# A gated projection split in twelve-bit parts: when its parts are made, and on which engine

## The chip, the cores and the metric

The kernel runs on one core of a Trainium2 chip. A core has five engines that matter here, each with its own queue of instructions in a fixed order: TensorE (PE in the profile; its weight loads are PEld), VectorE (DVE), ScalarE (ACT), GpSimd (POOL) and SyncE (SP), which issues transfers. TensorE multiplies from SBUF into the eight banks of PSUM; the others move and combine. The metric is the device time of one execution in microseconds (us), lower being better, given as the median of several runs.

## The reference

A graph network over 1024 nodes with 512 features: a normalisation, a graph convolution, four layers, a second graph convolution. What matters here is the second half of each layer:

```python
for i in range(L):                                    # L = 4
    a = _attn(_ln(h, ln2_w[i], ln2_b[i]), cond, Wq[i], Wk[i], Wv[i], Wo[i])
    h = h + a
    u = _ln(h, ln3_w[i], ln3_b[i]) @ geglu_w[i] + geglu_b[i]   # 1024x512 @ 512x4096
    val, gate = jnp.split(u, 2, axis=-1)
    f = val * jax.nn.gelu(gate, approximate=False)
    h = h + f @ ffo_w[i] + ffo_b[i]                            # 1024x2048 @ 2048x512
```

The first product, with `geglu_w`, is the gated projection; the second, with `ffo_w`, is the output product, and `ffo_w` holds the output weights.

## The kernel before

**Parts.** Most products are made in float32r, a matmul type for operands of few bits, in place of plain float32. So each operand is split in three: a high part (the value scaled by a power of two and rounded by the write), a low part (what is left), and a third part that is a combination of both. A product is then three matmuls: high by high and low by low into one bank, that bank scaled by `1 + TINY` on ScalarE or VectorE, and third by third on top.

**Seven products.** The gated projection is taken in blocks of 2 by 2 by a scheme with seven products in place of eight (0 to 6; `SPLIT` and `EARLY` are orders of these seven). The seven left operands are blocks of `geglu_w` and sums of blocks; the seven right operands (`right`) are blocks of the normalised, turned `h` (`ln3T`) and sums of them (`ln3S`). Value and gate halves of the weights are the two block rows, so that one run of seven products gives value and gate together.

**Order of the stage.** The columns of the projection are worked off in 16 units of 128. The first four are `Quad`s (L959), in plain float32, which need no parts. They run while the parts of the seven right blocks are made, one step at a time: `all_parts` (L1644) is a generator that goes over the blocks in the order `EARLY` = 0, 1, 4, 6, 5, 3, 2 and yields after every small step; `fill` (L1661) takes one step. A quad's `rest` (L987) calls its `fill` six times, between its sums on VectorE. For each block `begin_right` (L1022) makes the high part `gr` on ScalarE (L1024), twice a scaled half `gt` on ScalarE (L1027) and from it the third part, also `gr`, on VectorE (L1029); `finish_right` (L1032) makes the low part `gl` in two halves on VectorE (L1037). That is four steps a block.

The other twelve units are `Chunk`s (L1057). A chunk loads its weights (`gxa`, `gxb`), makes its sums of weight blocks on GpSimd (`sums`, L1073, instructions at L1079), and splits the weights (`split_steps`, L1081, through `split_left`, L1040): high parts `gha`, `ghb`, `gs` on ScalarE (L1042), low parts `gla`, `glb`, `gs` on VectorE (L1043), third parts `gsa`, `gsb`, `gs` on GpSimd (L1048). The "long" flow is the part of 128x1024 (`gha`, `gla`, `gsa`), the "short" flow the parts of 128x512 and 128x256. Then `steps` (L1136) does the seven products of three parts (L1107): for products 0, 5, 6 and 4 a scaling on ScalarE (L1121) stands between the second and the third part; for 1, 3 and 2 one on VectorE (L1125). The last steps of a chunk run inside the next chunk's iteration (`before`).

The loop over the chunks (from L1742) also prepares the stage behind it: `Output` (L1200) reads the result `f` back from DRAM (`fetch`), splits it (`split` through `left_parts`, L314: `ah_f` on ScalarE at L318, `al_f` on VectorE at L319, `as_f` on GpSimd at L321 for the first piece), and splits the output weights (`split_w`, L1223: `bh_wff` on ScalarE at L1226, `bl_wff` on VectorE at L1229, `bs_wff` on VectorE at L1233). `ahead` (L1237) runs `split_w` step by step: its first step comes at the end of the fifth chunk's iteration (`n == 0`), the next four in the chunks behind it, the rest in the output product (L1252).

**What sets the order.** A planner orders the instructions of each engine by program order as priority, by its own estimate of when operands and buffers are ready; it may put a later instruction ahead of an earlier one that has to wait. `pin` (L55) keeps pinned instructions in program order among themselves on their engine; `in_order` (L97) ties each instruction traced inside it behind the one traced before it on that engine. Buffers come from pools: 35 slots of 128x1024 (`slots`, L75), ten tiles of 128x512 (`work`, L76), and eight banks; a tile is given out again when its last reader is done.

**Last quad and first chunk.** Before the last quad's `rest`, the first chunk's two flows are begun (high parts), and that quad's six fills are taken from a list, `first_chunk` (L1710). The first chunk's sums are asked for after the second quad, the second chunk's after the third, and the third chunk's inside the first chunk's iteration, through `sum_next` (L1155).

Of the kernel before, what the change touches and what calls it, by code (L numbers as in the profile page):

```python
# [12 lines left out]
F32R = mybir.dt.float32r  # L13
I32 = mybir.dt.int32
AF = mybir.ActivationFunctionType
OP = mybir.AluOpType
# [5 lines left out]
TINY = 2.0 ** -12  # L22
INWARD = 1.0 - 2.0 ** -13
# [3 lines left out]
def gnn_kernel(  # L27
# [26 lines left out]
    nc = tc.nc  # L54
    pin = tc.keep_in_program_order  # L55
# [40 lines left out]
    @contextmanager  # L96
    def in_order(engine):  # L97

        traced = nc.cur_bb.bb.instructions
        n = len(traced)  # L100
        before = next((i for i in reversed(traced) if i.engine == engine), None)
        yield
        for i in traced[n:]:
            if i.engine == engine:
                if before is not None:
                    tc.add_manual_dep(i, before.name, mybir.DependencyInfo(
                        mybir.DependencyClass.NoSync, mybir.DependencyReason.DATA))
                before = i
# [4 lines left out]
    def t512(name, dtype=F32):  # L113
        return work.tile([P, 512], dtype, tag="t512", name=name)

    def slot(name):
        return slots.tile([P, 2, 512], F32, tag="slot", name=name)
# [109 lines left out]
    h = [hall[:, nb, :] for nb in range(NB)]  # L227
# [78 lines left out]
    def twelve_bits(t):  # L306
        return t.bitcast(F32R)
# [103 lines left out]
    def keys(l, g, wk, n=0, by=(0, 1)):  # L411

        to = blocks_in(kTs, g, f"kT_{l}_{g}")
        return [Twelve(f"k_{l}_{g}_{c}", wk, c, conds[g], to(c), by[c % 2]) for c in range(n, KC)]
# [59 lines left out]
    high = gp.tile([ET, P], F32, name="high")  # L474
# [543 lines left out]

    SPLIT = (0, 5, 6, 4, 1, 3, 2)
    EARLY = (0, 1, 4, 6, 5, 3, 2)  # L1020

    def begin_right(name, x, h, s):  # L1022

        nc.scalar.mul(h.bitcast(F32R), x, INWARD / TINY)  # L1024
        for k in range(2):
            more = t512(f"{name}_{k}")
            nc.scalar.mul(more, h[:, k, :], 1.0 + TINY)  # L1027
            yield
            pin(nc.vector.scalar_tensor_tensor(s.bitcast(F32R)[:, k, :], x[:, k, :], 1.0 / TINY,  # L1029
                                               more, OP.mult, OP.subtract))  # L1030

    def finish_right(name, x, h):  # L1032

        low = slot(name)
        for k in range(2):
            yield low
            pin(nc.vector.scalar_tensor_tensor(low.bitcast(F32R)[:, k, :], x[:, k, :], 1.0 / TINY,  # L1037
                                               h[:, k, :], OP.mult, OP.subtract))

    def split_left(x, h, l, s, t):  # L1040

        yield pin(nc.scalar.mul(h.bitcast(F32R), x, INWARD * TINY))  # L1042
        split_left.low = pin(nc.vector.scalar_tensor_tensor(l.bitcast(F32R), h, -1.0 / TINY, x,  # L1043
                                                            OP.mult, OP.add))
        yield split_left.low
        for at in range(0, x.shape[-1], 512):
            h_at, l_at, s_at = (t[:, at:min(at + 512, x.shape[-1])] for t in (h, l, s.bitcast(F32R)))
            split_left.last = pin(t.tensor_tensor(s_at, h_at, l_at, OP.subtract))  # L1048
            yield split_left.last
# [144 lines left out]
    def quads_of(l, r, left, right):  # L1194
        f = Gated(l, r)
        return f, [Quad(l, r, c, left, right, f) for c in range(KC)]
# [3 lines left out]
    class Output:  # L1200
# [22 lines left out]
        def split_w(self, u):  # L1223
            x, name = self.raw_w.pop(u), f"wff_{self.l}_{u}"
            h, l, s = self.w[u] = [slot(f"{n}_{name}") for n in ("bh", "bl", "bs")]
            nc.scalar.mul(twelve_bits(h), x, INWARD / TINY)  # L1226
            yield
            for k in range(2):
                pin(nc.vector.scalar_tensor_tensor(  # L1229
                    twelve_bits(l)[:, k, :], x[:, k, :], 1.0 / TINY, h[:, k, :], OP.mult,  # L1230
                    OP.subtract))
                yield
                pin(nc.vector.scalar_tensor_tensor(  # L1233
                    twelve_bits(s)[:, k, :], h[:, k, :], -TINY, l[:, k, :], OP.mult, OP.add))
                yield
# [155 lines left out]
    def four_wide(name):  # L1391
        return wos.tile([P, 4, 512], F32, tag="wos", name=name)
# [47 lines left out]
    for l in range(L):  # L1440
# [128 lines left out]
        for g in range(NG - 1):  # L1569
# [13 lines left out]
            k = keys(l, g + 1, wk, 1 if l == 0 and g == 0 else 0)  # L1583
# [55 lines left out]
        f, quads = quads_of(l, 0, left, right)  # L1639
# [4 lines left out]
        def all_parts():  # L1644
            for i in EARLY:
                x, name = right[i], f"{l}_{i}"
                if i == 3:
                    wide = four_wide(f"gr_{l}")
                    high, mid = wide[:, :2, :], wide[:, 2:, :]
                else:  # L1650
                    high, mid = slot(f"gr_{name}"), slot(f"gr_{name}")
                yield from begin_right(f"gt_{name}", x, high, mid)
                flow = finish_right(f"gl_{name}", x, high)
                Chunk.rights[i] = high, next(flow), mid
                yield
                for _ in flow:
                    yield

        parts = all_parts()

        def fill(n=1):  # L1661
# [35 lines left out]
        def load():  # L1697
            if chunks:
                ready.append(Chunk(l, *chunks.pop(0)))

        def sum_chunk(n):
            if n < len(ready):
                ready[n].sums()

        def begin_split(n, low, t=nc.gpsimd):
            flow = ready[n].split_steps(low, t) if n < len(ready) else iter(())
            next(flow, None)
            return flow

        first_chunk = []  # L1710
# [5 lines left out]
        for c, q in enumerate(quads):  # L1716
            if c == KC - 1:
                long, short = (begin_split(0, low) for low in (False, True))
                first_chunk.extend([[long] * 3, [short], [short] * 4, [parts], [parts], [parts]])
            q.rest(fill_first if c == KC - 1 else fill)  # L1720
            if c == 0:
                load()
            if c == 1:
                sum_chunk(0)
                load()
            if c == 2:
                sum_chunk(1)
                load()

        def split_rest(short):  # L1730
            long = begin_split(0, False)
            next(long, None)
            with waiting_for(split_left.low, mybir.EngineType.Pool):
                for flow in short, long:
                    for _ in flow:
                        pass

        output = Output(l)
        ahead = output.ahead()
        before, short = None, iter(())  # L1740
        for r in range(1, R):
            f = Gated(l, r)  # L1742
            for c in range(KC):
                n = (r - R + 2) * KC + c
                if n == -1:
                    output.fetch_w(0)
                if (r, c) == (R - 1, KC - 2):
                    output.fetch(0)
                chunk = ready.pop(0)
                flow = chunk.steps(lambda: sum_chunk(1))  # L1750
                chunk.f = f
                next(flow)
                if 0 < n < 5:
                    next(ahead)
                for _ in islice(short, 2):
                    pass
                next(flow)
                if before:
                    split_rest(short)
                    load()  # L1760
                for _ in parts:
                    pass
                if (r, c) == (R - 1, KC - 1):
                    output.split(0, nc.gpsimd)
                    output.fetch(1)
                for step in range(3):
                    if before:
                        next(before, None)
                    next(flow)
                    if step == 1 and not before:  # L1770
                        split_rest(iter(()))
                        load()
                before = flow
                short = begin_split(0, True)
                if n == 0:
                    next(ahead)
# [204 lines left out]
```

## Time and profile before

| | us |
|---|---|
| median of 3 runs | 2312.76 (2312.65 to 2314.91) |
| the profiled execution | 2312.2 |
| its span, first to last instruction | 2310.4 |

| engine | busy, share of the span |
|---|---|
| PE | 99% |
| PEld, DVE | 75% each |
| ACT | 48% |
| POOL | 32% |

The granted TensorE clock was 1.000 over the span. Lines of a timeline give the start in us from the span's start, the duration in us (of all merged instructions), engine, source line, operation, output<-inputs, size and count, and in brackets the idle time of the engine just before with what ended it. Successive matmuls overlap: two of 128x512 last 0.62 us together but the next two start 0.455 later, so lost time is read from starts, not from ends. A row of waits gives the total us, how often, and the longest. A row of windows gives a stretch, its length, then for PE, PEld, DVE, ACT and POOL busy time (instructions), the granted clock, the share of the DMA engines and GB/s. A row of the profile's groups gives the busy time and mean ns of one.

### The profile page before, as it was taken

Reading aid. Unit: us, or ns where it says so; the run is one execution under the profiler, and the core shown is the slowest. Engines: PE = TensorE matmul, PEld = TensorE weight load, DVE = VectorE, ACT = ScalarE, POOL = GpSimd, SP = SyncE. Lnnn points to the kernel's source line nnn. Section 1 sums busy time; section 2 is a strip of 40 time slices with the busy share of each in tenths; the row PEclk is TensorE's granted clock in tenths of the full one; section 3 lists DMA queues with packets and bytes.
Section 4 is the critical chain, followed back from the end, with each engine's and each line's share of the span. In section 5 each row is a group of like instructions: output and inputs, shape, how many; then the busy total and the mean of one; then the engine's idle time right before and its main releaser. Section 6 shows DMA issues by size and latency. Waiting matters only on the chain. (4 is left out here: it accounts for less than half of the span.)

```text
span 2310.4 us, 34068 instructions
## 1 busy us (share of the span) xinstructions
PE 2277.8 (99%) x12352; PEld 1727.6 (75%) x12352; DVE 1723.2 (75%) x3208; ACT 1118.5 (48%) x2175; POOL 732.3 (32%) x647
## 2 busy tenths in 40 slices
PE   8999999999999999999999999999999999999999
PEld 4667887587877887477886888578886888668777
DVE  9876556998976456989986554989987554889964
ACT  7544545565345445455344444556335444556410
POOL 1132223385031124277022222278122113168311
PEclk9999999999999999999999999999999999999999
DMA  7042120245411101243522111133531011033551
GB/s 214 2 151 87 55 87 10 78 119 168 160 64 56 46 29 38 59 124 106 204 82 74 37 38 37 42 110 96 191 137 58 35 46 47 13 116 110 182 191 38
DMA packets 160496, 204.40 MB, mean 88 GB/s; under 512 B 11241, under 2 KB 101681, under 8 KB 160321
## 3 DMA queue, kind: packets, MB, share of 16 engines
q1 hardware_dynamic: 158224, 196.72, 26.4%
q0 software_dynamic: 1376, 4.30, 0.6%
q8 instruction: 102, 1.67, 0.3%
q10 hardware_dynamic: 720, 1.11, 0.1%
q14 instruction: 74, 0.60, 0.1%
HBM read 151.75 MB, written 50.34 MB: 87 GB/s over the span
## 5 line engine op out<-in xcount | busy, mean ns | idle before, releaser
L324 POOL TENSOR_TENSOR as_c<-ah_c,al_c 128x512 fp32r<-128x512 f32 x128 | 200.4, 1595 | 913.0 <-DVE al_c L319 708.5
L1121 ACT ACTIVATE g<-g 128x512 f32<-128x512 f32 x192 | 112.5, 586 | 151.3 <-PE g L1107 151.0
L381 ACT ACTIVATE k<-k 128x512 f32<-128x512 f32 x125 | 72.8, 585 | 218.4 <-PE k L370 218.4
L1252 PE MATMUL fx<-bs_wff,as_f 128*128 128x512 f32 x512 | 158.8, 390 | 0.6 <-DVE as_f L321 0.6
L1252 PE MATMUL fy<-bl_wff,al_f 128*128 128x512 f32 x512 | 158.8, 390 | 0.5 <-DVE al_f L319 0.5
L1252 PE MATMUL fy<-bh_wff,ah_f 128*128 128x512 f32 x512 | 157.9, 389 | 0.2 <-ACT ah_f L318 0.2
L386 DVE COPY kT<-k 128x512 f32<-128x512 f32 x54 | 37.2, 688 | 159.1 <-PE k L370 159.1
L318 ACT ACTIVATE ah_f<-fr 128x1024 fp32r<-128x1024 f32 x64 | 67.9, 1061 | 178.7 <-PE fy L1252 99.5
L370 PE MATMUL v<-bs_wv,as_c 128*128 128x512 f32 x508 | 137.7, 393 | 3.1 <-ACT v L381 3.1
L370 PE MATMUL v<-bh_wv,ah_c 128*128 128x512 f32 x508 | 140.7, 399 | 0.0
L851 ACT ACTIVATE pr<-sc,nmax 128x256 f32<-128x256 f32 x256 | 118.2, 474 | 46.0 <-DVE nmax L846 45.5
L370 PE MATMUL v<-bl_wv,al_c 128*128 128x512 f32 x508 | 136.3, 390 | 0.0
L1048 POOL TENSOR_TENSOR gsa<-gha,gla 128x512 fp32r<-128x512 f32 x96 | 124.2, 1317 | 34.3 <-DVE gla L1043 23.0
L370 PE MATMUL k<-ah_c,bh_wk 128*128 128x512 f32 x500 | 135.0, 392 | 0.0
L370 PE MATMUL k<-al_c,bl_wk 128*128 128x512 f32 x500 | 133.7, 389 | 0.0
L381 ACT ACTIVATE v<-v 128x512 f32<-128x512 f32 x127 | 75.0, 591 | 119.0 <-PE v L370 116.9
L370 PE MATMUL k<-as_c,bs_wk 128*128 128x512 f32 x500 | 132.3, 395 | 0.0
L1107 PE MATMUL g<-gr,gsa 128*128 128x512 f32 x384 | 121.3, 397 | 7.0 <-ACT g L1121 7.0
L1107 PE MATMUL g<-gr,gha 128*128 128x512 f32 x384 | 120.0, 394 | 0.0
L1107 PE MATMUL g<-gl,gla 128*128 128x512 f32 x384 | 118.3, 389 | 0.0
L370 PEld LDWEIGHTS v<-bh_wv,ah_c 128*128 128x128 f32 x508 | 92.6, 188 | 27.9 <-issue 9.3
L370 PEld LDWEIGHTS v<-bs_wv,as_c 128*128 128x128 f32 x508 | 93.2, 188 | 27.0 <-ACT v L381 4.8
(340 smaller groups left out, 5705.3 us busy)
## 6 DMA issues: line engine op xcount, KB each, us to landing
f_dram<-fT SPq DMA_DIRECT2D x128, 256.0 KB, 2.7
fr<-f_dram SPq DMA_DIRECT2D x64, 512.0 KB, 4.3
ct<-cond_dram SPq DMA_DIRECT2D x48, 512.0 KB, 4.4
wff<-in_L_gnn_ffo_w_dram SPq DMA_DIRECT2D x32, 512.0 KB, 5.8
gxb<-in_L_gnn_geglu_w_dram SPq DMA_DIRECT2D x96, 128.0 KB, 2.7
gxa<-in_L_gnn_geglu_w_dram SPq DMA_DIRECT2D x96, 128.0 KB, 2.7
cond<-in_L_gnn_cond_dram SPq DMA_DIRECT2D x32, 256.0 KB, 4.4
cond_dram<-ct SPq DMA_DIRECT2D x16, 512.0 KB, 3.3
```

The costliest lines, as they stand in the source:

```text
L318: nc.scalar.mul(twelve_bits(h), x, INWARD * TINY)
L324: nc.gpsimd.tensor_tensor(twelve_bits(s)[:, k, :], h[:, k, :], l[:, k, :], OP.subtract)
L370: pin(nc.tensor.matmul(self.bank, twelve_bits(left[k // 2])[:, k % 2, self.c * P:(self.c + 1) * P], twelve_bits(right[k // 2])[:, k % 2, : ...
L381: nc.scalar.mul(self.bank, self.bank, 1.0 + TINY)
L386: nc.vector.tensor_copy(self.to(), self.bank)
L851: nc.scalar.activation(pr3[:, a, :], ps3[:, a, :], AF.Exp, bias=nmax[:, a:a + 1], accum_out=tot[:, a:a + 1])
L1048: split_left.last = pin(t.tensor_tensor(s_at, h_at, l_at, OP.subtract))
L1107: pin(nc.tensor.matmul(to, self.part(i, which)[:, k, :], self.rights[i][which].bitcast(F32R)[:, k, :], start=start and k == 0, stop=stop a ...
L1121: pin(nc.scalar.mul(to, to, 1.0 + TINY))
L1252: pin(nc.tensor.matmul(to, twelve_bits(left[which][0])[:, k, b * P:(b + 1) * P], twelve_bits(right[which])[:, k, :], start=u == 0 and whic ...
```

## The change

- `split_w` pins the high part of the output weights.
- For right blocks 4 and 6 a new generator, `right_beside`, takes the place of `begin_right` and `finish_right`: ScalarE makes the high part and two scaled halves (by `TINY`), VectorE the low part in halves, and GpSimd the third part as low part minus scaled half. It has two steps a block where the others have four.
- In the last quad the list of fills begins with one step of the right parts, then the first chunk's long low and third parts, then its short ones; the last two fills are empty.
- The third chunk's sums are asked for right after the last quad, and the first chunk's iteration asks for none.
- The split of the first piece of `f` is tied in order on ScalarE, VectorE and GpSimd.

```diff
     EARLY = (0, 1, 4, 6, 5, 3, 2)
+    BESIDE = (4, 6)
...
+    def right_beside(name, x, h, s):
+
+        low = slot(f"gl_{name}")
+        nc.scalar.mul(h.bitcast(F32R), x, INWARD / TINY)
+        less = [t512(f"gt_{name}_{k}") for k in range(2)]
+        for k in range(2):
+            nc.scalar.mul(less[k], h[:, k, :], TINY)
+        for k in range(2):
+            yield low
+            pin(nc.vector.scalar_tensor_tensor(low.bitcast(F32R)[:, k, :], x[:, k, :], 1.0 / TINY,
+                                               h[:, k, :], OP.mult, OP.subtract))
+            pin(nc.gpsimd.tensor_tensor(s.bitcast(F32R)[:, k, :], low[:, k, :], less[k],
+                                        OP.subtract))
...
         def split_w(self, u):
-            nc.scalar.mul(twelve_bits(h), x, INWARD / TINY)
+            pin(nc.scalar.mul(twelve_bits(h), x, INWARD / TINY))
...
                     high, mid = slot(f"gr_{name}"), slot(f"gr_{name}")
+                if i in BESIDE:
+                    flow = right_beside(name, x, high, mid)
+                    Chunk.rights[i] = high, next(flow), mid
+                    yield
+                    for _ in flow:
+                        yield
+                    continue
...
-                first_chunk.extend([[long] * 3, [short], [short] * 4, [parts], [parts], [parts]])
+                first_chunk.extend([[parts], [long] * 3, [short], [short] * 4, [], []])
...
             if c == 2:
                 sum_chunk(1)
                 load()
+        sum_chunk(2)
...
-                flow = chunk.steps(lambda: sum_chunk(1))
+                flow = chunk.steps(lambda: before and sum_chunk(1))
...
                 if (r, c) == (R - 1, KC - 1):
-                    output.split(0, nc.gpsimd)
+                    with in_order(mybir.EngineType.Activation), in_order(mybir.EngineType.DVE), \
+                            in_order(mybir.EngineType.Pool):
+                        output.split(0, nc.gpsimd)
                     output.fetch(1)
```

## The prediction

> **What bounds the kernel now.** I read the busy shares first, then what TensorE (PE) waited for, then its timeline.
>
> ```profile
> PE 2277.8 (99%) x12352; PEld 1727.6 (75%) x12352; DVE 1723.2 (75%) x3208; ACT 1118.5 (48%) x2175; POOL 732.3 (32%) x647
> ```
> ```profile
> PE g L1107 <- ACT g L1121: 7.0, 12, 0.8
> ...
> PE gc L301 <- DVE gu L995: 3.3, 4, 0.9
> ```
>
> PE sets the end: it is busy all but 1% of the time, so a change that adds and removes no matmul can only win PE's waits or add new ones. The two rows come three times and once per layer: 12 and 4 times over 4 layers. The first is TensorE waiting for a scaling `(1 + TINY)` of a bank on ScalarE (ACT) in the chunks, the second for a sum on VectorE (DVE) in the last quad. Layer 0 shows what each costs, as the first matmuls of successive chunks, with the three waits between them:
>
> ```profile
> 454.12 0.62 PE L1107 MATMUL g<-gr,gha 128*128 128x512 f32 x2
> ...
> 460.49 0.70 PE L1107 MATMUL g<-gr,gsa 128*128 128x512 f32 x2 [0.30 <-ACT g L1121]
> ...
> 464.51 0.62 PE L1107 MATMUL g<-gr,gha 128*128 128x512 f32 x2
> ...
> 474.12 0.62 PE L1107 MATMUL g<-gr,gha 128*128 128x512 f32 x2
> ...
> 483.72 0.61 PE L1107 MATMUL g<-gr,gha 128*128 128x512 f32 x2
> ...
> 491.88 0.73 PE L1107 MATMUL g<-gr,gsa 128*128 128x512 f32 x2 [0.72 <-ACT g L1121]
> ...
> 494.28 0.61 PE L1107 MATMUL g<-gr,gha 128*128 128x512 f32 x2
> ...
> 542.26 0.62 PE L1107 MATMUL g<-gr,gha 128*128 128x512 f32 x2
> ...
> 550.46 0.73 PE L1107 MATMUL g<-gr,gsa 128*128 128x512 f32 x2 [0.77 <-ACT g L1121]
> ...
> 552.87 0.62 PE L1107 MATMUL g<-gr,gha 128*128 128x512 f32 x2
> ```
>
> Undisturbed chunks take 9.61 and 9.60 us (464.51 to 474.12 to 483.72). The three with a wait take 10.39, 10.56 and 10.61, which is 0.79, 0.96 and 1.01 too much: 2.76 in this layer. Its three waits are 0.30 + 0.72 + 0.77 = 1.79 of the 7.0 in all, so four layers count as 7.0 / 1.79 = 3.9 of this one.
>
> The quads, by their first product and the last quad's late one:
>
> ```profile
> 409.59 1.88 PE L301 MATMUL gb<-ln3S,ges 128*128 128x512 f32 x4
> ...
> 418.17 1.88 PE L301 MATMUL gb<-ln3S,ges 128*128 128x512 f32 x4
> ...
> 426.97 1.88 PE L301 MATMUL gb<-ln3S,ges 128*128 128x512 f32 x4
> ...
> 435.87 1.88 PE L301 MATMUL gb<-ln3S,ges 128*128 128x512 f32 x4
> ...
> 439.30 1.88 PE L301 MATMUL gd<-ln3S,ges 128*128 128x512 f32 x4
> ...
> 442.07 1.98 PE L301 MATMUL gc<-ln3S,wgate 128*128 128x512 f32 x4 [0.89 <-DVE gu L995]
> ```
>
> A free quad takes 8.58, or 1.72 a product. The next two take 8.80 and 8.90 (0.22 and 0.32 lost), and the last loses 442.07 - 439.30 - 1.72 = 1.05: together 1.59 a layer.
>
> **Part A, `bh_wff` tied (the pin in `split_w`).** Nothing is added or removed; one ScalarE instruction moves.
>
> ```profile
> 490.28 1.05 ACT L1226 ACTIVATE bh_wff<-wff 128x1024 fp32r<-128x1024 f32 x1
> 491.23 0.59 ACT L1121 ACTIVATE g<-g 128x512 f32<-128x512 f32 x1
> ...
> 495.39 0.58 ACT L1121 ACTIVATE g<-g 128x512 f32<-128x512 f32 x1 [2.71 <-PE g L1107]
> ```
>
> Now it runs ahead of the scaling that PE waits for at 491.88. In program order it is traced behind that scaling and the next chunk's short high parts, so the pin puts it where ScalarE is idle for 2.71 us before 495.39. It takes 1.05 and ends some 1.7 before the next scaling. Its first reader, `bl_wff`, is traced behind that chunk's first scaling. Gain 0.96. Without the idle stretch the wait would only move one chunk on. The later `bh_wff` come after the last chunk, where nothing else pinned on ScalarE is left to order them: 0.
>
> **Part C, `output.split(0)` in order.** `ah_f`, `al_f` and `as_f` move on ScalarE, VectorE and GpSimd (POOL).
>
> ```profile
> 548.87 1.06 ACT L318 ACTIVATE ah_f<-fr 128x1024 fp32r<-128x1024 f32 x1
> ...
> 555.84 0.59 ACT L1150 COPY gs<-g 128x512 f32<-128x512 f32 x1 [0.38 <-PE g L1107]
> ```
> ```profile
> 496.79 1.05 ACT L1042 ACTIVATE gha<-gxa 128x1024 fp32r<-128x1024 f32 x1
> ```
> ```profile
> 554.84 1.22 DVE L319 SCALAR_TENSOR_TENSOR al_f<-ah_f,fr 128x1024 fp32r<-128x1024 f32 x1
> ...
> 557.94 0.75 DVE L1173 SCALAR_TENSOR_TENSOR fT<-g,gcols,g 128x512 f32<-128x512 f32 x1 [1.88 <-ACT g L1134]
> ```
> ```profile
> 557.87 2.40 POOL L321 TENSOR_TENSOR as_f<-ah_f,al_f 128x1024 fp32r<-128x1024 f32 x1
> ```
>
> `ah_f` is ahead of a scaling at 548.87; the tie puts it behind the last chunk's second scaling, which ends at 555.84 - 0.38 = 555.46. There it stands as `gha` (1.05) stands in an ordinary chunk, such as the one from 494.28, that loses nothing; the copy behind it starts some 0.7 later, as it does there. `al_f` (1.22) follows at 556.5 and ends near 557.8, in the 1.88 that VectorE idles before 557.94, and `as_f` starts near 557.9, where it already does. Gain 1.01. If that idle were gone, the last chunk's sums on VectorE would be late by up to 1.2.
>
> **Part D, the third chunk's sums sooner.**
>
> ```profile
> 458.32 1.06 ACT L1042 ACTIVATE gha<-gxa 128x1024 fp32r<-128x1024 f32 x1 [1.55 <-POOL gxa L1079]
> ```
> ```profile
> 452.61 2.55 POOL L1048 TENSOR_TENSOR gsa<-gha,gla 128x512 fp32r<-128x512 f32 x2 [5.60 <-DVE gla L1043]
> ```
> ```profile
> 439.39 1.10 SPq L1069 DMA_DIRECT2D gxa<-in_L_gnn_geglu_w_dram  x2
> ```
> ```profile
> gxa<-in_L_gnn_geglu_w_dram SPq DMA_DIRECT2D x96, 128.0 KB, 2.7
> ```
>
> The wait at 460.49 begins with `gha` of the third chunk, which stands 1.55 for sums that run behind the `gsa` of 452.61. The four sums go ahead of that `gsa`, into the 5.60 that GpSimd idles before it, and the weights they need were issued at 439.39 and land 2.7 later. `gha` then follows the scaling before it at once. No transfer moves. If the sums reach into `gsa`, it comes a little late for a PE that wants it near 456. Gain 0.79.
>
> **Part B, two blocks' third parts on GpSimd, and the last quad's fills.** Four VectorE instructions a layer go and four GpSimd ones come; each block keeps its ScalarE work (one high part, two half-size products). A block of the new kind takes two fill steps, not four, so every later step is taken four fills sooner, and each fill of the quads still holds one VectorE instruction: the four are saved after the quads, where PE does not wait for them. What GpSimd does to VectorE meanwhile decides:
>
> ```profile
> 441.50 2.95 POOL L1048 TENSOR_TENSOR gsa<-gha,gla 128x512 fp32r<-128x512 f32 x2 [2.96 <-DVE gla L1043]
> ```
> ```profile
> 422.10 0.68 DVE L1037 SCALAR_TENSOR_TENSOR gl<-ln3S,gr 128x512 fp32r<-128x512 f32 x1
> 422.70 0.68 DVE L995 TENSOR_TENSOR gu<-gc,gu 128x512 f32<-128x512 f32 x1
> ...
> 440.21 1.21 DVE L1043 SCALAR_TENSOR_TENSOR gla<-gha,gxa 128x1024 fp32r<-128x1024 f32 x1
> ...
> 441.94 1.37 DVE L1043 SCALAR_TENSOR_TENSOR glb<-ghb,gxb 128x512 fp32r<-128x512 f32 x1
> ...
> 443.23 0.68 DVE L995 TENSOR_TENSOR g<-gd,gu 128x512 f32<-128x512 f32 x1
> ```
> ```profile
> 409.59:445.39 35.80, 34.87 (x82) 14.71 (x80) 33.08 (x50) 18.11 (x26) 11.05 (x12) 1.00 0.30 88
> ```
>
> A part read from SBUF alone takes 0.68 by itself, and 1.37 when it starts 0.44 into a GpSimd instruction: it ended some 0.55 after that one's 1.27 (2.55 / 2), then GpSimd's second half ran. The add of 443.23 reads a bank and kept its 0.68. So a GpSimd third part costs VectorE what is left of its 1.27 when the next SBUF instruction is due, and nothing beside adds. VectorE has little room: 33.08 busy in 35.80, or 0.68 free a quad.
>
> Set out by hand on the old starts, with VectorE going on 0.60 after an instruction: the first third part falls at 418.0, beside adds and the products with the gate, and is free. The other three fall from 421.5 on, each behind a low part, alternate with VectorE's parts and hold up three of them by some 0.65: the sum of 422.70 comes at 423.3, and the quad leaves VectorE near 1.9 late, of which its room takes 0.7. PE then waits some 0.7 in the second quad where it lost 0.22, and 0.7 in the third (0.32). In the last quad the fill ahead of the late sum is a low part of 0.68 in place of `gla` with 1.21, which leaves 0.5 of the 1.05. Sum 1.9 against 1.59, or 0.3 lost; I take 0.2, since the third quad could keep some of its room. The last block's three buffers are wanted four fills sooner too, while by the code some 34 of the 35 slots are held; no row prices a wait there, and I leave it to the range. The bounds: if all four fall beside adds, the quads' whole 1.59 is won; if each holds VectorE up for a whole 1.27, that is 5.1 less 2.0 of room less the 0.5, or 2.6 lost.
>
> The Trainium skill, "SBUF — State Buffer", section "Who interferes with whom", says that a VectorE instruction with two SBUF inputs and a GpSimd one that reads SBUF exclude each other, and that the second to issue fully blocks. The rows above agree (1.37 beside 0.68). Read at its hardest, four whole waits, the rule speaks against this part: that is the first rival below, whose time by rows is 2312.1.
>
> **The sum.** A layer gains 0.96 + 1.01 + 0.79 - 0.2 = 2.56; times 3.9 that is 10.0. The profiled execution took 2312.2 (span 2310.4, 1.8 around it); the median of the runs is 2312.76, 0.56 above. So 2312.76 - 10.0 = 2302.8.
>
> **Rivals.**
> - *GpSimd holds VectorE up four whole times.* B loses 2.6: 2312.76 - 3.9 x (2.76 - 2.6) = 2312.1, no change. For: the three late ones come in a row. Against: 1.37, not 1.95.
> - *Slower: GpSimd keeps the port through its queue.* Were VectorE let in only once GpSimd's queue is empty, two third parts (2.5) and then one with the first chunk's four sums (1.27 + 3.0) would stand before a low part: 6.8 less 2.5 of room and swap, 4.3 a layer, 2312.76 + 3.9 x (4.3 - 2.76) = 2318.8. It decides from 2.76 a layer. Against: `glb` got in between the halves of `gsa`.
> - *The port costs nothing.* B wins 1.59: 2312.76 - 3.9 x 4.35 = 2295.8. For: inside a quad all but the last two parts have a bank's add or a product with the gate behind them. Against: the second quad is where three third parts meet VectorE without a gap.
> - *The ties move the waits, not remove them* (the change doesn't do what it says): if the two ScalarE parts only delay the next scaling, D and B remain: 2312.76 - 3.9 x 0.59 = 2310.5, no change. Against: the 2.71 of idle, and `gha` in the same place.
>
> **Chances.** Forecast 0.66, free port 0.14, four whole waits 0.07, moved waits 0.06, port kept 0.07. A measurement of this kernel tells a change from none at about 0.2%, or 4.6 us: faster 0.80, same 0.13, slower 0.07. The range from 2295.5 to 2309.5 takes in the free port and stops short of the rest; 2299 to 2307 is the forecast's own.
>
> **What would show it.** Three waits on L1121 per layer gone (7.0 to under 1); `bh_wff` behind the chunk's short high part; `ah_f` behind the last chunk's second scaling; sums ahead of the second chunk's `gsa`. B right: the late product of the second and third quad waits some 0.7, the last 0.5, and low parts beside GpSimd take about 1.25. The forecast is wrong if chunks still differ by over 0.5, or if the quads lose under 0.8 or over 3 a layer.

## The result and the profile after

| | before | after |
|---|---|---|
| median of 9 runs each, on one chip, us | 2314.91 (2312.46 to 2316.75) | 2306.11 (2304.26 to 2310.59) |
| the profiled execution, us | 2312.2 | 2304.26 |
| its span, at a granted clock of 1.000, us | 2310.4 | 2302.3 |

The ratio of the medians is 0.9966, with an interval of 0.9956 to 0.9976: 0.34% faster. The forecast was 2302.8, in a range from 2295.5 to 2309.5. The forecast started from 2312.76, while the kernel before took 2314.91 beside these runs, so it is the drop that can be compared: 8.8 us, where 10.0 was forecast. Of the nine runs after, the four at a granted clock of 1.000 took 2304.26 to 2305.83 and the two at 0.998 took 2308.89 and 2310.59, so below I compare the lengths of stages in the traces rather than medians wherever less than 5 us is in question.

The page's row of PE and two rows of what PE waited for, after the change (total us, times, longest):

```profile
PE 2274.3 (99%) x12352; PEld 1728.4 (75%) x12352; DVE 1721.4 (75%) x3192; ACT 1119.1 (49%) x2175; POOL 757.8 (33%) x663
```
```profile
PE gc L301 <- DVE gu L995: 4.4, 8, 0.7
...
PE g L1122 <- DVE g L1140: 1.3, 4, 0.3
```

(Lines from 1040 to about 1650 have moved by 15, some before them by 1, later ones by more; L1050 and L1052 are the new low and third parts. The chunks' matmuls are L1122, the scalings L1136 on ScalarE and L1140 on VectorE, `sums` L1094, the three splits L1057, L1058 and L1063, `bh_wff` L1241, `bl_wff` L1244, `bs_wff` L1248.) PE has the same 12352 matmuls; VectorE has 16 instructions fewer, GpSimd 16 more. The twelve waits on ScalarE's scalings, 7.0 us before, are gone altogether. A wait of the same kind on VectorE has come, once a layer; late quad products are two a layer where there was one.

PE's timeline of layer 0, first matmuls of chunks, and the new wait:

```profile
454.48 0.61 PE L1122 MATMUL g<-gr,gha 128*128 128x512 f32 x2
...
464.04 0.61 PE L1122 MATMUL g<-gr,gha 128*128 128x512 f32 x2
...
483.16 0.61 PE L1122 MATMUL g<-gr,gha 128*128 128x512 f32 x2
...
492.72 0.61 PE L1122 MATMUL g<-gr,gha 128*128 128x512 f32 x2
...
540.89 0.61 PE L1122 MATMUL g<-gr,gha 128*128 128x512 f32 x2
...
550.54 0.62 PE L1122 MATMUL g<-gr,gha 128*128 128x512 f32 x2
...
561.03 0.73 PE L1122 MATMUL g<-gr,gsb 128*128 128x512 f32 x2 [0.32 <-DVE g L1140]
```

The three chunks that took 10.39, 10.56 and 10.61 take 9.56, 9.56 and 9.65. The last chunk, with the new wait of 0.32, is longer than it was. The quads of the same layer:

```profile
409.93 1.88 PE L301 MATMUL gb<-ln3S,ges 128*128 128x512 f32 x4
...
418.51 1.88 PE L301 MATMUL gb<-ln3S,ges 128*128 128x512 f32 x4
...
427.80 1.88 PE L301 MATMUL gb<-ln3S,ges 128*128 128x512 f32 x4
...
433.80 1.98 PE L301 MATMUL gc<-ln3S,wgate 128*128 128x512 f32 x4 [0.68 <-DVE gu L995]
...
437.33 1.88 PE L301 MATMUL gb<-ln3S,ges 128*128 128x512 f32 x4
...
440.77 1.88 PE L301 MATMUL gd<-ln3S,ges 128*128 128x512 f32 x4
...
442.59 1.98 PE L301 MATMUL gc<-ln3S,wgate 128*128 128x512 f32 x4
```

A free quad still takes 8.58. The second takes 9.29 and the third 9.53 (0.71 and 0.95 lost), the last loses 442.59 - 440.77 - 1.72 = 0.10. So the loss has moved from the last quad to the two in the middle.

To compare kernels I use the length of three stages, from starts: the quads from the first product `gb` to the chunks' first matmul, the chunks from there to the output product's first matmul, the output product to its end. From layer to layer the chunks repeat within 0.15 us (in one kernel below the last layer's took 0.5 longer) and the quads within 0.1, but for a stage that differs by 0.1 to 0.4 now and then; the output product varies by up to 0.8 between the layers of one kernel. Means over the four layers, worked out from the traces (the output product over the first three; but for one kernel below, the last layer's took 89.8 where the granted clock of that stage was 1.00, and 91.4 where it was 0.98):

| kernel | quads | chunks | output product | span |
|---|---|---|---|---|
| before | 35.65 | 118.82 | 87.62 | 2310.4 |
| after | 35.81 | 116.54 | 87.69 | 2302.3 |

Chunks give 2.28 a layer, quads take 0.16, the output product some 0.07 in three layers: 4 x 2.12 - 0.2 = 8.3, of the 8.1 by which the spans differ.

### The profile page after: what moved, and what is told of

Same layout as the page of the kernel before. It is cut to its first block, busy times and chain, and to the rows that moved or that the text cites. A ratio compares the mean times of both kernels' runs of the same rounds, so it can differ in the third digit from the quotient of the medians.

```text
span 2302.3 us, 34093 instructions
## 1 busy us (share of the span) xinstructions
PE 2274.3 (99%) x12352; PEld 1728.4 (75%) x12352; DVE 1721.4 (75%) x3192; ACT 1119.1 (49%) x2175; POOL 757.8 (33%) x663
## 5 line engine op out<-in xcount | busy, mean ns | idle before, releaser
L1136 ACT ACTIVATE g<-g 128x512 f32<-128x512 f32 x192 | 112.5, 586 | 152.5 <-PE g L1122 150.8
L1063 POOL TENSOR_TENSOR gsa<-gha,gla 128x512 fp32r<-128x512 f32 x96 | 124.2, 1316 | 40.5 <-DVE gla L1058 40.5
L1122 PE MATMUL g<-gr,gha 128*128 128x512 f32 x384 | 119.9, 394 | 0.0
L1122 PE MATMUL g<-gr,gsa 128*128 128x512 f32 x384 | 119.9, 393 | 0.0
L1122 PE MATMUL g<-gl,gla 128*128 128x512 f32 x384 | 118.3, 389 | 0.0
```

The costliest lines, as they stand in the source:

```text
L1122: pin(nc.tensor.matmul(to, self.part(i, which)[:, k, :], self.rights[i][which].bitcast(F32R)[:, k, :], start=start and k == 0, stop=stop a ...
L1136: pin(nc.scalar.mul(to, to, 1.0 + TINY))
```

## The experiments

**Each part alone.** Four kernels are the kernel before with one part of the change each.

The pin alone:

```diff
-            nc.scalar.mul(twelve_bits(h), x, INWARD / TINY)
+            pin(nc.scalar.mul(twelve_bits(h), x, INWARD / TINY))
```

> The kernel before with the pin in split_w alone. Theory: the high part of the output weights leaves the place ahead of the scaling and finds 2.7 us of idle ScalarE behind the chunk's short high parts, so four of the twelve waits on L1121 go and each layer gains 0.96 us: 3.7 us less (0.16%). Rival (the tie only moves the wait one chunk on): still twelve waits, 0 to 0.5 us less.

The tie alone:

```diff
-                    output.split(0, nc.gpsimd)
+                    with in_order(mybir.EngineType.Activation), in_order(mybir.EngineType.DVE), \
+                            in_order(mybir.EngineType.Pool):
+                        output.split(0, nc.gpsimd)
```

> The kernel before with output.split(0) tied in order alone. Theory: the wait of 1.0 us in the eleventh chunk goes, but the low part of f now starts while GpSimd makes the short third parts, takes about 1.9 us in place of 1.2 and makes TensorE wait some 0.4 us for VectorE (the scaling L1125) in the last chunk: 0.6 a layer, 2.5 us less. Rival (the last chunk's new wait comes from TensorE being earlier by the whole change, not from this tie): no wait of 0.3 us in the last chunk, 3.9 us less.

The sums alone:

```diff
+        sum_chunk(2)
...
-                flow = chunk.steps(lambda: sum_chunk(1))
+                flow = chunk.steps(lambda: before and sum_chunk(1))
```

> The kernel before with the third chunk's sums right after the last quad, alone. Theory: the second chunk's wait on L1121 (0.79 us a layer) goes, 3.1 us less. Rival (the sums stand ahead of the second chunk's third parts on GpSimd and these come late for TensorE): the wait is replaced by one for gsa, 0 to 1 us less.

The right blocks and the list of fills alone (with `right_beside` and its call as in the change):

```diff
+    BESIDE = (4, 6)
...
-                first_chunk.extend([[long] * 3, [short], [short] * 4, [parts], [parts], [parts]])
+                first_chunk.extend([[parts], [long] * 3, [short], [short] * 4, [], []])
```

> The kernel before with the two blocks' third parts on GpSimd and the last quad's new list of fills, alone. Theory: low and third parts of VectorE that meet a GpSimd third part take 1.15 to 1.25 us in place of 0.68; the second and third quads lose 0.7 and 0.95 us in place of 0.2 and 0.3, the last 0.2 in place of 1.05: 0.2 a layer lost, about 0.8 us more, no change that can be measured. Rival (the four instructions less on VectorE are worth their time): 4 x 0.6 us a layer in the stage, up to 6 us less.

Measured, against 2313.02 for the kernel before (31 runs on that chip):

| alone | median, us | ratio | quads | chunks | chunks won | predicted |
|---|---|---|---|---|---|---|
| A, pin | 2312.78 | 1.000 (0.9991 to 1.001) | 35.59 | 118.75 | 0.07 | 0.96 |
| C, tie | 2311.74 | 0.9993 (0.9983 to 1.0002) | 35.63 | 118.14 | 0.68 | 1.01 |
| D, sums | 2307.76 | 0.9975 (0.9966 to 0.9985) | 35.70 | 117.41 | 1.41 | 0.79 |
| B, blocks and fills | 2310.02 | 0.9986 (0.9977 to 0.9996) | 35.83 | 117.91 | 0.91 | 0 |

Only B's quads came as predicted (0.18 lost). In the chunks no part alone wins what the prediction gave it (the tie wins about the 0.6 that was expected of it alone by then), and the four add up to 3.07 where together they win 2.28. The pin is the strangest: it removes its wait (four of the twelve are gone, 4.1 us are left of 7.0) and wins nothing. That kernel's row of waits, and its ScalarE timeline:

```profile
PE g L1107 <- ACT g L1121: 4.1, 8, 0.8
```
```profile
486.94 1.06 ACT L1042 ACTIVATE gha<-gxa 128x1024 fp32r<-128x1024 f32 x1 [0.79 <-POOL gxa L1079]
...
491.41 1.06 ACT L1226 ACTIVATE bh_wff<-wff 128x1024 fp32r<-128x1024 f32 x1
...
496.55 1.06 ACT L1042 ACTIVATE gha<-gxa 128x1024 fp32r<-128x1024 f32 x1 [0.80 <-POOL gxa L1079]
...
506.36 1.06 ACT L1042 ACTIVATE gha<-gxa 128x1024 fp32r<-128x1024 f32 x1 [1.00 <-POOL gxa L1079]
...
516.16 1.06 ACT L1042 ACTIVATE gha<-gxa 128x1024 fp32r<-128x1024 f32 x1 [1.02 <-POOL gxa L1079]
```

From the third chunk's on, every `gha` in it stands waiting for GpSimd's sums. In layer 0 the spacings of the first matmuls are:

| chunk | 2 | 3 | 4 | 5 | 6 | 7 | 8 | 9 | 10 | 11 | 12 |
|---|---|---|---|---|---|---|---|---|---|---|---|
| before | 10.39 | 9.61 | 9.61 | 10.56 | 9.56 | 9.56 | 9.56 | 9.56 | 9.74 | 10.61 | 11.35 |
| A alone | 10.38 | 9.59 | 9.61 | 9.59 | 9.59 | 9.80 | 9.80 | 9.82 | 9.87 | 10.61 | 11.35 |
| D alone | 9.56 | 9.56 | 9.56 | 10.11 | 9.56 | 9.56 | 9.56 | 9.56 | 9.66 | 10.59 | 11.35 |
| B alone | 9.59 | 9.58 | 9.60 | 10.54 | 9.56 | 9.56 | 9.56 | 9.56 | 9.69 | 10.59 | 11.36 |
| after | 9.56 | 9.56 | 9.56 | 9.56 | 9.56 | 9.56 | 9.56 | 9.63 | 9.86 | 9.65 | 11.72 |

So 9.56 is PE's own pace, and the 9.61 that the prediction took for an undisturbed chunk was already 0.05 over it. What the pin alone wins in chunk 5 (0.97) is lost again in chunks 7 to 10, 0.24, 0.24, 0.26 and 0.13 more than before. Each follows a chunk in which a step of the output weights (`bl_wff`, `bs_wff`) runs on VectorE. The same kernel's VectorE and GpSimd in chunk 7, which has such a step, and VectorE in chunk 5, which has none:

```profile
504.72 1.01 DVE L1233 SCALAR_TENSOR_TENSOR bs_wff<-bh_wff,bl_wff 128x512 fp32r<-128x512 f32 x1
...
507.68 1.21 DVE L1043 SCALAR_TENSOR_TENSOR gla<-gha,gxa 128x1024 fp32r<-128x1024 f32 x1
```
```profile
508.97 1.30 POOL L1048 TENSOR_TENSOR gsb<-ghb,glb 128x512 fp32r<-128x512 f32 x1 [1.49 <-DVE gla L1043]
```
```profile
488.04 1.22 DVE L1043 SCALAR_TENSOR_TENSOR gla<-gha,gxa 128x1024 fp32r<-128x1024 f32 x1 [0.84 <-ACT gha L1042]
```

The chunks' preparation is a ring over three engines: ScalarE's `gha`, VectorE's `gla`, GpSimd's third parts and then its sums for the chunk after, and from those sums the next `gha`. One turn: `gha` at 506.36, `gla` 1.32 later, `gsb` 1.29 after that, the next `gha` at 516.16, 7.19 after `gsb`: 9.80. In a chunk without a step `gla` stands idle for `gha` and starts 488.04 - 486.94 = 1.10 after it, and the turn is 496.55 - 486.94 = 9.61. With a step ahead of it VectorE comes to `gla` 0.22 later, and the turn is longer by about that (0.19). PE can't run faster than this ring for long, only ahead of it by what the ring has in hand: how early `gha` follows the chunk's first scaling. Before, the wait for `bh_wff` held PE up by 0.9 while GpSimd went on; this was the head start from which chunks 6 to 9 ran at 9.56. The kernel before shows it being used up: its `gha` of 506.55 has no listed idle time ahead of it, and the next two stand waiting again, longer each time:

```profile
516.38 1.06 ACT L1042 ACTIVATE gha<-gxa 128x1024 fp32r<-128x1024 f32 x1 [0.38 <-POOL gxa L1079]
...
526.20 1.06 ACT L1042 ACTIVATE gha<-gxa 128x1024 fp32r<-128x1024 f32 x1 [0.64 <-POOL gxa L1079]
```

Without the head start PE is held back in each of these chunks.

D alone won more than predicted for the same reason: the sums come early, which gives the ring a head start from chunk 2 on, and the wait for `bh_wff` is halved (10.11 for 10.56). B alone, given nothing in the chunks, removed the whole wait of chunk 2: with VectorE's four instructions gone from there `gsa` starts 0.16 sooner, the second and third of the sums behind it take 1.88 in place of 2.35, and `gha` starts at 457.69 where it started at 458.32. B and D thus remove the same wait.

**The ring put to the test.** Two more kernels are the kernel before with parts: the pin with the sums; and the pin with the four VectorE steps of the output weights left out of the chunks, so that they run in the output product.

```diff
-                if 0 < n < 5:
-                    next(ahead)
```

> The kernel before with the pin in split_w and the sooner sums, nothing else. Theory (a ring of ScalarE's gha, VectorE's gla, GpSimd's third parts and sums, which needs about 9.6 us a chunk, and 9.8 in the four chunks that also take a step of the output weights, beside TensorE's 9.56; the sums sooner give it a head start and each such chunk eats some 0.24 of it): the tie takes the 0.54 us of the fifth chunk away and the ring gives 0.3 to 0.5 of it back in the chunks behind, so a layer gains 0.1 to 0.3 over the sums alone, 0.4 to 1.2 us. Rival (the parts add): 0.5 to 1 a layer over the sums alone, 2 to 4 us.

> The kernel before with the pin in split_w, and with the four VectorE steps of the first output weights taken out of the chunks: they fall due at the start of the output product. Theory (ring): without these steps the four chunks of 9.8 us that stand in the kernel with the pin alone go back to 9.6, so the chunks lose some 0.9 us a layer less than with the pin alone; the output product then begins with waits for bl_wff and bs_wff of 1 to 3 us a layer, and the time is longer. Rival (these chunks lose their 0.2 for another reason): they still take 9.8.

The pin with the sums took 2307.95 against 2312.8 (0.998, 0.9971 to 0.9989), chunks 117.51 where the sums alone have 117.41: the pin adds nothing to them either, where the ring was expected to leave it 0.1 to 0.3 a layer. Chunks 2 to 7 take 9.56, then 9.75, 9.83 and 9.88. The head start from the sums (`gha` 1.46 after the scaling in the second chunk, 1.97 by the sixth) lasts to chunk 7 and is then used up. With the steps moved out, the chunks take 117.80, which is 0.95 less than with the pin alone, for the 0.9 expected; chunks 3 to 10 take 9.57 to 9.61 with no step between them: without the four instructions the turn is 9.6 throughout. The output product then waits for the weights instead, and is 7.2 a layer longer than before where 1 to 3 was expected, so the kernel took 2337.67 (one run, at a granted clock of 0.994):

```profile
PE fy L1252 <- DVE bl_wff L1229: 19.5, 8, 4.3
```

In the kernel after, the sums and the lighter VectorE together give the ring enough. Its `gha` starts with no listed idle time ahead of it (under 0.1) up to the one of the sixth chunk, and drifts by 0.25 a chunk from there, until the row of 534.70 waits about as long as in the kernel with the pin alone (1.10):

```profile
485.81 1.06 ACT L1057 ACTIVATE gha<-gxa 128x1024 fp32r<-128x1024 f32 x1
...
490.59 1.05 ACT L1241 ACTIVATE bh_wff<-wff 128x1024 fp32r<-128x1024 f32 x1
...
495.40 1.06 ACT L1057 ACTIVATE gha<-gxa 128x1024 fp32r<-128x1024 f32 x1
505.22 1.06 ACT L1057 ACTIVATE gha<-gxa 128x1024 fp32r<-128x1024 f32 x1 [0.35 <-POOL gxa L1094]
...
534.70 1.06 ACT L1057 ACTIVATE gha<-gxa 128x1024 fp32r<-128x1024 f32 x1 [1.08 <-POOL gxa L1094]
```

**The kernel after without GpSimd's third parts.** `BESIDE = (4, 6)` becomes `BESIDE = ()`, so that VectorE makes all third parts again, with the new list of fills; and the same on top of the experiment on the last chunk below.

> The changed kernel with all seven right blocks by the old helpers (no third part of them on GpSimd); the last quad's list of fills, the ties and the sums stay. Theory (GpSimd's hold on VectorE costs the second and third quad their waits): these lose 0.2 and 0.3 us as before, the last quad 0.5 since a low or third part of 0.68 stands there in place of gla, so a layer gains 1.77 - 1.05 = 0.7 over the changed kernel, 2 to 3 us less than it. Rival (the shorter list of steps is what lets the last quad go free): the last quad waits 1.0 again and the time is that of the changed kernel.

> Both: no third part of right blocks on GpSimd, and the last chunk's third parts behind al_f. Theory: the gains add, about 4 us less than the changed kernel, span near 2298. Rival: one gives the other back, no better than the better of the two alone.

The first took 2309.91 against 2313.23 (0.9985, 0.9976 to 0.9994): quads 35.03, which is 0.78 shorter than after, as expected, but chunks 118.08, 1.54 longer, so that it is slower than after and not faster. The last quad takes only one step of the right parts, so one block's parts come in the first chunk, beside GpSimd's sums, and the second chunk's `gla` behind them:

```profile
449.66 2.42 DVE L1030 SCALAR_TENSOR_TENSOR gr<-ln3T,gt 128x512 fp32r<-128x512 f32 x2
452.00 2.37 DVE L1038 SCALAR_TENSOR_TENSOR gl<-ln3T,gr 128x512 fp32r<-128x512 f32 x2
...
454.89 1.21 DVE L1058 SCALAR_TENSOR_TENSOR gla<-gha,gxa 128x1024 fp32r<-128x1024 f32 x1
```

Chunks 2 and 3 take 10.15 and 9.74 and chunks 4 to 10 take 9.59 to 9.85: the head start is gone. The other kernel took 2308.91 (0.998, 0.9971 to 0.9989), span 2306.6 and not the 2298 expected, where the same with GpSimd's third parts has 2303.3. So with these parts the quads are 0.8 a layer longer (not all of it by VectorE being held up, as the next experiment shows), and they are worth it: 3.3 us net.

**What the port costs in the quads.** The third parts of blocks 4 and 6 give way to a memset of GpSimd in one kernel (the first line added below), to a ScalarE copy of the scaled half in the other (the second).

```diff
-            pin(nc.gpsimd.tensor_tensor(s.bitcast(F32R)[:, k, :], low[:, k, :], less[k],
-                                        OP.subtract))
+            pin(nc.gpsimd.memset(s[:, k, :], TINY))
+            nc.scalar.mul(s.bitcast(F32R)[:, k, :], less[k], 1.0)
```

> The changed kernel with the four third parts a layer left out: GpSimd fills their place with a constant instead, reading nothing from SBUF. Theory (port): the VectorE parts of the second quad take 0.68 again and that quad loses 0.2 us in place of 0.7; the third quad loses 0.3 to 0.6 in place of 0.95, since GpSimd's sums of the second chunk still meet VectorE there. Rival (the steps taken sooner load the quads, whatever GpSimd does): 0.7 and 0.95 as in the changed kernel.

> The changed kernel with the four third parts a layer left out of GpSimd: ScalarE writes a copy of the scaled half into their place, so the sum with the low part is left out. Every step stays where the change puts it, only GpSimd's work beside VectorE is gone. Theory (the port): low parts beside them take 0.68 again and the quads lose under 0.4 us a layer in place of 1.77, span some 5 us shorter than the changed kernel's 2302.3. Rival (the steps taken sooner load the second and third quad): they still lose 0.7 and 0.95 us, span within 1 us of 2302.3.

GpSimd and VectorE in the second quad of the kernel after, and VectorE in the third:

```profile
421.46 4.95 POOL L1052 TENSOR_TENSOR gr<-gl,gt 128x512 fp32r<-128x512 f32 x3 [1.73 <-DVE gl L1050]
...
430.21 1.17 POOL L1094 TENSOR_TENSOR gxa<-gxa,gxb 128x256 f32<-128x256 f32 x1
```
```profile
422.44 1.17 DVE L1050 SCALAR_TENSOR_TENSOR gl<-ln3T,gr 128x512 fp32r<-128x512 f32 x1
423.53 0.68 DVE L995 TENSOR_TENSOR gu<-gc,gu 128x512 f32<-128x512 f32 x1
424.13 1.15 DVE L1030 SCALAR_TENSOR_TENSOR gr<-ln3S,gt 128x512 fp32r<-128x512 f32 x1
425.21 0.68 DVE L995 TENSOR_TENSOR g<-gd,gu 128x512 f32<-128x512 f32 x1
425.81 1.16 DVE L1030 SCALAR_TENSOR_TENSOR gr<-ln3S,gt 128x512 fp32r<-128x512 f32 x1
...
430.73 1.21 DVE L1030 SCALAR_TENSOR_TENSOR gr<-ln3S,gt 128x512 fp32r<-128x512 f32 x1
```

Three parts beside three third parts take 1.16 where 0.68 is usual, the adds between them 0.68. With the memset in their place these parts take 0.69, as expected, and the second quad's late product is no longer late; PE and VectorE of that kernel:

```profile
423.68 1.98 PE L301 MATMUL gc<-ln3S,wgate 128*128 128x512 f32 x4
...
433.41 1.98 PE L301 MATMUL gc<-ln3S,wgate 128*128 128x512 f32 x4 [0.89 <-DVE gu L995]
```
```profile
429.34 1.09 DVE L1038 SCALAR_TENSOR_TENSOR gl<-ln3S,gr 128x512 fp32r<-128x512 f32 x1
430.35 1.21 DVE L1030 SCALAR_TENSOR_TENSOR gr<-ln3S,gt 128x512 fp32r<-128x512 f32 x1
```

But its third quad still waits 0.89, where 0.3 to 0.6 was expected. What holds VectorE up there is not the third parts but the sums of the second chunk, on GpSimd from 430.21 after and from 429.84 here. They ran from 435.18 before, because SyncE issued their weights behind the store of `f`, `gxa` at 430.44 and `gxb` after it; after, it issues this `gxa` at 425.67, ahead of the store. Part B alone moves them too (from 431.18). The same sums, and a part that VectorE makes beside them, before:

```profile
435.18 1.05 POOL L1079 TENSOR_TENSOR gxa<-gxa,gxb 128x256 f32<-128x256 f32 x1 [5.85 <-DMA gxb<-in_L_gnn_geglu_w_dram]
...
437.80 0.73 POOL L1079 TENSOR_TENSOR gy<-gxb,gxa 128x256 f32<-128x256 f32 x1
```
```profile
437.99 1.09 DVE L1029 SCALAR_TENSOR_TENSOR gr<-ln3S,gt 128x512 fp32r<-128x512 f32 x1
```

So before, they took 0.4 from the last quad. Now that they run sooner, they take it from the third and leave the last free. The kernel without GpSimd's third parts shows this price by itself: its last quad loses 0.5 in the three layers where a part of it takes 1.1 beside the sums, and 0.17 in the layer where none does. The quads are 35.54 with the memset and 35.81 after, so the third parts' hold on VectorE costs 0.27 a layer (0.48 in the second quad, less the 0.21 more that the third loses without them). (2305.78, one run; span 2303.9, of which some 1.6 is its last output product at a granted clock of 0.98.) The memsets ran before 412, and so say nothing on an instruction that only writes. The ScalarE copy brought quads of 35.60 and a span of 2302.9 (2304.79, one run), the rival's figure and not the 5 us expected, but VectorE then waited up to 0.65 for ScalarE, so it tells little on the port. Neither is shown to beat the kernel after.

**The wait in the last chunk.** The tie alone and the kernel after have the same new wait of 0.3 a layer; VectorE and GpSimd after:

```profile
554.14 1.93 DVE L319 SCALAR_TENSOR_TENSOR al_f<-ah_f,fr 128x1024 fp32r<-128x1024 f32 x1 [0.59 <-ACT ah_f L318]
```
```profile
553.68 1.30 POOL L1063 TENSOR_TENSOR gsb<-ghb,glb 128x512 fp32r<-128x512 f32 x1 [2.37 <-DVE gs L1058]
554.94 1.72 POOL L1063 TENSOR_TENSOR gs<-gs 128x256 fp32r<-128x256 f32 x1
```

`al_f` reads two tiles in SBUF and becomes ready 0.46 into GpSimd's `gsb`; it takes 1.93 for 1.22, and GpSimd's next, `gs`, 1.72 for 0.74. The Trainium skill, "SBUF — State Buffer", section "SBUF: two separate sides", says that of a VectorE instruction with two SBUF inputs and a GpSimd one that reads SBUF, whichever starts first gets the ports they share for its whole instruction, and the other is blocked. The trace agrees, in both directions here: `al_f` ends 1.09 after `gsb`, and `gs` 0.59 after `al_f`, a little less than each takes alone. To take the collision away, the last chunk's short third parts are made to wait for `al_f`:

```diff
-                        output.split(0, nc.gpsimd)
...
+                        nc.scalar.mul(twelve_bits(fh[0]), fr, INWARD * TINY)
+                        first_low = nc.vector.scalar_tensor_tensor(
+                            twelve_bits(fl[0]), fh[0], -1.0 / TINY, fr, OP.mult, OP.add)
+                    with waiting_for(first_low, mybir.EngineType.Pool), \
+                            in_order(mybir.EngineType.Pool):
+                        for _ in short:
+                            pass
+                        nc.gpsimd.tensor_tensor(twelve_bits(fs[0]), fh[0], fl[0], OP.subtract)
```

> The changed kernel with GpSimd's short third parts of the last chunk made to wait for the low part of f. Theory: al_f takes 1.22 us in place of 1.93, the four waits of 0.3 us on L1140 go, 0.4 us a layer: about 1.5 us less than the changed kernel, span near 2300.8. Rival (the last chunk's chain on VectorE is the bound by itself): the waits stay, no difference.

`al_f` took 1.23, the wait is gone and the chunks take 116.27, 0.27 less than after. The output product takes 88.34 in the first three layers, 0.65 more; the waits have a new row there, 0.3 for `bl_wff`, which is only a part of it. The span is 2303.3 against 2302.3, the median 2306.74 (0.9969, 0.9956 to 0.9981): no gain, where 1.5 us was expected. What the output product waits for is a piece of `f` read back from DRAM. Its second `ah_f` in layer 0, after and in this kernel:

```profile
568.57 1.06 ACT L318 ACTIVATE ah_f<-fr 128x1024 fp32r<-128x1024 f32 x1 [3.57 <-DMA fr<-f_dram]
```
```profile
568.78 1.06 ACT L318 ACTIVATE ah_f<-fr 128x1024 fp32r<-128x1024 f32 x1 [4.07 <-DMA fr<-f_dram]
```

The chunks end 0.29 sooner in that layer, but the piece is there no sooner. In the first three layers of every kernel here but the one with the steps left out, a start of this `ah_f` up to 6.1 us after the beginning of the output product costs nothing, and each 0.1 beyond that makes the stage 0.1 longer, within some 0.04. It starts 6.07 after that beginning in the kernel after and 6.82 in this one (means), so the loss of 0.65 is this wait. Why the piece comes later stays open.

**Sums ahead of the long third parts.** The ring would be shorter if GpSimd made the next sums ahead of `gsa`.

```diff
+                for _ in short:
+                    pass
+                if sums:
+                    sum_chunk(1)
+                for _ in long:
+                    pass
```

> The changed kernel with each chunk's sums on GpSimd ahead of the long third parts instead of behind them, so that the ring is some 2.5 us shorter. Theory (ring): gha no longer drifts behind the chunk's first scaling but stays near 1.4 to 1.6 us in all chunks, the waits in the tenth and eleventh chunk go, 0.3 to 0.7 us a layer, 1 to 3 us less than the changed kernel. Rival (VectorE alone is the limit in these chunks): gha drifts as before and the time stays, or TensorE waits for gsa, which comes later, and the time grows.

`gha` no longer drifts, as expected: it starts 1.40 after the scaling in every chunk from the third on. But `gsa` is now last on GpSimd, and PE waits for it instead:

```profile
PE g L1122 <- POOL gsa L1063: 3.3, 12, 0.3
```

Chunks 8 to 10 take 10.17, 10.16 and 10.13; the stage takes 117.78, 1.24 longer than after. It took 2310.77 (0.9991, 0.9982 to 1.0), slower than after: the second half of the rival came true.

## Why the prediction was right, and where its steps were not

- *The total.* 2.56 a layer was forecast, 2.12 came (chunks 2.28 for 2.76, quads -0.16 for -0.2). Over the layers 10.0 was forecast and the spans differ by 8.1. The sign, the bound (PE's waits) and the three waits in the chunks were right: chunks 2, 5 and 11 are 0.83, 1.00 and 0.96 shorter, for 0.79, 0.96 and 1.01.
- *Part A, "Gain 0.96".* Its placement came true: `bh_wff` runs at 490.59 in ScalarE's idle time and delays nothing. Its price did not hold by itself. Alone it wins 0.07, with the sums -0.10. The step that failed is the reading of a chunk with a wait as a free chunk plus a wait: chunks 6 to 9 were "free" only because of the wait. The prediction's "without the idle stretch the wait would only move one chunk on" looked at ScalarE's queue; the wait was spread over four later chunks through GpSimd's ring. The rival "the ties move the waits, not remove them" describes the pin by itself, though by this way and not by the next scaling. In the kernel after the wait is gone and chunks 6 to 8 still take 9.56; I put that down to the head start that B and D bring in place of the wait, from the idle times ahead of `gha`, but no run takes the pin alone out of the kernel after.
- *Part B, "the four are saved after the quads, where PE does not wait for them".* This is the sentence that was wrong: alone they are worth 0.91 a layer in the chunks, and without them the kernel after loses 1.54 there. The price in the quads, 0.7, 0.7 and 0.5, came as 0.71, 0.95 and 0.10, a sum of 1.76 for 1.9. That the sum came so near is in part luck: the second quad is as worked out, but the third quad's loss and the last quad's 0.4 less are the second chunk's sums, which run sooner, not a lack of room. Part B's working has no term for them; the prediction's "No transfer moves" stands in part D, on the third chunk's weights. The rivals of a whole hold and of a port kept through the queue fell with the parts of 1.16.
- *Part D, "Gain 0.79".* The wait it names was removed as worked out. Alone it is worth 1.41, since the sums made early also give head start.
- *Part C, "Gain 1.01".* The term that was mis-sized: `ah_f` went where it was put and chunk 11 won 0.96, but chunk 12 lost 0.37 (11.72 for 11.35). `al_f` was costed at 1.22 and takes 1.93; it was checked against VectorE's idle time and not against GpSimd's third part beside it. Alone the tie wins 0.68.
- The rest of the chunks' 0.48: 2.76 forecast, plus 0.10 in chunks 3 and 4, plus 0.03 over the three waits, less 0.37 in chunk 12 and 0.19 in chunks 9 and 10, where the head start ends, is 2.33; layer 0 measured 118.83 - 116.52 = 2.31.

The additive sum came near since A and C were priced too high by themselves and B and D too low, and the gains of B and D overlap; that the errors met is luck and no proof of the sum. On top of the sums alone (117.41) the three other parts together win only 0.87 a layer in the chunks, where the prediction gave them 1.97.

## What to carry to other kernels

When an engine that sets the end is fed by a loop over other engines, compare the loop's own period with its pace before pricing a wait: a wait removed is won only if the loop has slack, and otherwise it comes back as smaller losses too short to be listed as waits. Read those from the starts of equal stages, and the slack from the idle time ahead of the first instruction of the loop. A part moved into idle time of its own engine must also be checked against what shares a port with it at that moment. A stage that ends sooner wins only if the next one's input, here a piece read back from DRAM, is there sooner too.

## What the runs showed of the hardware

The prediction's row of 1.37 for 0.68 was one collision, 0.69 too long. The runs show others. `al_f`, 128x1024, took 1.93 for 1.22 after it met a `gsb` 0.46 old, and it delayed GpSimd's `gs` from 0.74 to 1.72. In the first chunk of the kernel without GpSimd's third parts, pairs of VectorE parts took 2.42 and 2.37 beside GpSimd's sums, where a pair took 1.28 before. In the second quad after, three GpSimd third parts took 4.95 together where one alone takes 1.27, and the VectorE parts among them 1.15 to 1.17 for 0.68. So in a queue of such instructions on both engines each one pays, not only the first. VectorE's adds with one input in a bank kept 0.68 beside the same work.
